# Two-step transfers, whole left slabs and a projection in 64x64 tiles, in a two-layer banded convolution kernel

## The chip, the cores and the metric

The kernel runs on one core of a Trainium2 chip. The metric is the device time of one execution in microseconds (us); lower is better. A core has five engines that run side by side, each through its own list of instructions in order: TensorE (PE, matrix products into PSUM), VectorE (DVE), ScalarE (ACT), GpSimd (POOL) and SyncE (SP, which here issues nearly all DMA transfers). They meet at semaphores only. SBUF is the on-chip memory with 128 partitions; x, the output and some intermediate arrays are in DRAM.

## The reference

x has the shape 1 x 512 x 512 x 64, float32. Two layers of the same form follow each other. Cut to what matters, one layer is (written as `_ln` for a normalization over the last axis, here without scale and bias since these are folded into weights):

```python
xn = _ln(x)                                             # over 64 channels
left  = (xn @ Wl + bl) * mask * sigmoid(xn @ Wlg + blg)  # 128 hidden channels
right = (xn @ Wr + br) * mask * sigmoid(xn @ Wrg + brg)
gate  = sigmoid(xn @ Wog + bog)
out[i, j] = sum over d = -4..4 of left[i + d, i] * right[i + d, j]
out = _ln(out) * gate
result = out @ Wo + bo
```

`left` is needed only in a band of nine entries around the diagonal. Around the layers the whole function also has a group normalization of the layer's input (statistics over the whole picture) and a residual, so that each layer reads its input twice: once as z, to be normalized, and once as XR, to which the result is added.

## The kernel before, in words

**Blocks and steps.** The 512 rows are cut into nine overlapping blocks of 64 rows (56 or 60 of them are kept, `blk.m`). The columns of a block are worked in two halves at once: partitions 0 to 63 hold the block's rows for a column of the left half, partitions 64 to 127 the same rows for a column of the right half. One step takes 8 columns of each half (`JU`), 16 steps make a chunk (`NU`), 18 chunks a layer, so a layer has 288 steps and 30 more in which its pipeline runs empty. In the function `layer` a step's item list (`FIRST` for the first layer, `SECOND` for the second) says in which order each engine gets its work; nothing is reordered inside an engine.

**One step.** z (128 partitions x 8 columns x 64 channels) is loaded two steps or more ahead (`load`), scaled and moved by the group normalization and centred (POOL), its row statistics are taken (DVE), it is transposed on PE (`transposed`, bank <- ident,z) and copied from PSUM to a tile `zT` on ACT (`kept`, line 477). `zT` has two buffers. It is used twice. First in the next step by PE for the projection to `right` (`crossed`, line 507; zT and pack are its operands): ACT makes the sigmoid of the gate half (`sg`) and DVE multiplies it into `RO`, the array of right. Second, `zT` is stored to DRAM (`later`), and read back as `zg` for the output gate of the step 30 further on. The band product (`mix`, RO and A as operands, output again to RO) has an operand A, a slab of 16 hidden channels of left that is fetched from DRAM (`take_left`, line 586); three slab buffers exist. A layer has as many band products as steps; within 16 steps they stand in the first ten, one or two a step. Then come the statistics of the band result (DVE), the normalization (`on`, ACT and two or fewer columns on POOL), its transposition, the gate (zg, pack -> `gate`, ACT), the product with it (`times_gate`, to `ZH`, DVE), the last product (`end`, PE), the sum with XR (`ended`, DVE), and the store. In the first layer PE also sums the results for the next group normalization (`sums`, acc <- XR).

**PE's tiles.** PE runs these products in different divisions of its array, which the profile prints as rows*columns: the gate, the projection and both transpositions in 64*128 (two products side by side), the last product and the sums in 128*64, the band products in 64*64 (four side by side). An f32 product shows as two matmul records, a transposition as one.

**What crosses in the projection.** `crossed` exchanges the two column halves for every second pair of 64 hidden channels, so that the band product finds its operands in the right partitions. It does so by reading `zT` from column 64 on for s = 1; for this `kept` writes the first 64 columns of each 192-column group a second time (the third third, `to[:, 2]`).

**Transfers.** All of them are issued by SP, in order, one after another: per step z (2 transfers, `load` line 405), later (1), zg (1), XR (2, `fetch` line 764), store of the result (2, `ended` line 788), and four for a slab A in every second step on average. In the first layer also some that prepare the left array (`left_of`). Eight completion semaphores are used in turn, so that a transfer is issued only when the one eight places before it has landed. One transfer moves 64 or 128 rows; `later` reads pieces of 512 B from zT, A and XR are moved in pieces of 512 B, z and zg in pieces of 2 KB.

Of the kernel before, what the change touches and what calls it, by code (L numbers as in the profile page):

```python
# [17 lines left out]
P = 128  # L18
# [86 lines left out]
def tile_two_banded_layers(  # L105
# [39 lines left out]
    ones_row = const.tile([1, P], F32, name="ones_row")  # L145
    nc.vector.memset(ones_row, 1.0)
# [93 lines left out]
    def solve_layer(i: int, f: dict, r: dict, tmp, half: bass.AP):  # L240
# [10 lines left out]
        for nm, lo, hi in (("right", 0, 2), ("left", 2, 4), ("gate", 4, 5)):  # L251
# [7 lines left out]
            en.vector.tensor_tensor(r[nm], aug[:, lo:hi], pm, ALU.subtract)  # L259
            en.vector.tensor_tensor(r[nm], r[nm], pb, ALU.add)  # L260
# [56 lines left out]
    both = const.tile([P, 2 * D], F32, name="both")  # L317
    total = const.tile([P, G], F32, name="total")

    fewer = const.tile([P, 2 * D], F32, name="fewer")  # L320
# [8 lines left out]
    def input_stats(meanwhile):  # L329
# [4 lines left out]
        with tc.tile_pool(name="gnx", bufs=3) as gx, tc.tile_pool(name="gns", bufs=1) as gs:  # L334
# [24 lines left out]
            tot = total  # L359
# [34 lines left out]
    zp = ctx.enter_context(tc.tile_pool(name="zp", bufs=11))  # L394
# [10 lines left out]
    def load(src: bass.AP, u: Unit):  # L405
        u.z = zp.tile([P, JU, D], F32, tag="z", name="z")
        if u.near is None:
            rows = slice(u.blk.s, u.blk.s + S)
            for e, j in enumerate((u.j, LH + u.j)):
                en.sync.dma_start(u.z[e * S : (e + 1) * S], src[rows, j : j + JU, :])  # L410
            return
        spans = [(0, u.near, u.near + JU)]
# [64 lines left out]
    def kept(u: Unit):  # L477
        u.t = ztp.tile([P, JU // 2, P + S], F32, tag="zT", name="zT")
        to = u.t.rearrange("c k (n p) -> c n k p", n=3)
# [106 lines left out]
    def take_left(n: int, h: int) -> bass.AP:  # L586


        A = lp.tile([P, HA // 2, S, 2], F32, tag="A", name="A")
        q = HA // 4  # L590
        for e in range(2):
            for s in range(2):
                en.sync.dma_start(
                    A[e * S : (e + 1) * S, s * q : (s + 1) * q].rearrange("p h i t -> p h (i t)"),
                    strided(
                        left_of, n * size + (s * H // 4 + h * q) * span + 2 * WIN,
                        (H // 2 * span, S), (span, q), (1, 2 * S),
                    ),
                )
        return A  # L600
# [37 lines left out]
    def solve(w: dict, ins: list, outs: list, sti, sto) -> dict:  # L638
# [3 lines left out]
        r = sm.tile([P, 3 * NB], F32, tag="rs", name="rs", bufs=3)[:, :n]  # L642
# [12 lines left out]
        def temporary(tag: str):  # L655
            return sm.tile([P, 3 * NB], F32, tag=tag, name=tag, bufs=1)[:, :n]
# [71 lines left out]
    def gated(o: Out):  # L728
        b = o.blk
        n = 2 * JQ * b.m  # L730
# [6 lines left out]
        o.g = g[:, : 2 * n].rearrange("h (x n p) -> h n x p", n=2, p=b.m)  # L737
# [14 lines left out]
    def times_gate(o: Out, w: dict):  # L752
        b = o.blk
        for n, pt in enumerate(o.pt):
            en.vector.scalar_tensor_tensor(
                ZH[(2 * o.n + n) % len(ZH)][:, :, : b.m], pt[:, :, b.lo : b.hi], w["ob"],
                o.g[:, n], ALU.add, ALU.mult,
            )

    def rows_of(v: bass.AP, o: Out, e: int):  # L760
        b, j = o.blk, e * LH + o.j
        return v[b.s + b.lo : b.s + b.hi, j : j + JU, :].rearrange("p (k t) c -> p k (t c)", t=2)

    def fetch(src: bass.AP, o: Out, w: dict, n: int):
        o.n, o.xr = n, XR[n % len(XR)]
        for e in range(2):
            en.sync.dma_start(o.xr[e * S : e * S + o.blk.m, :, 1 : 1 + 2 * D], rows_of(src, o, e))

    def biased(o: Out, w: dict):
        n = S + o.blk.m  # L770
        f = o.xr[:n, :, 1 : 1 + 2 * D]
        add = fewer if o.blk.m < S - WIN else both
        en.gpsimd.tensor_tensor(f, f, mid(add[:n], JU // 2), ALU.add)

    def end(o: Out, w: dict):
        po = one_bank().rearrange("i (j c) -> i j c", c=D)
        for k in range(JQ):
            for e in range(2):
                for n in range(2):
# [3 lines left out]
                        lhsT=ZH[(2 * o.n + n) % len(ZH)][:, e * JQ + k, :], rhs=w["Wo"],  # L783
# [4 lines left out]
    def ended(dst: bass.AP, o: Out):  # L788
        m, po = o.blk.m, o.po
        f = o.xr[: S + m, :, 1 : 1 + 2 * D]  # L790
# [3 lines left out]
        for e in range(2):  # L794
            en.sync.dma_start(rows_of(dst, o, e), o.xr[e * S : e * S + m, :, 1 : 1 + 2 * D])
# [13 lines left out]
    def layer(src: bass.AP, dst: bass.AP, w: dict, stats: bool, then=None):  # L809
# [64 lines left out]
        early = [u for t in sorted(loads) for u in loads[t] if u.near is None and u.at < 7]  # L874
        for u in early:
            load(src, u)
# [275 lines left out]
```

## Time and profile before

| | |
|---|---|
| time, median of 3 runs | 4618.48 us (4608.68 to 4629.22) |
| the profiled execution's own time | 4606.09 us |
| its span, first to last instruction | 4603.0 us |
| PE / its weight loads / DVE / ACT / POOL busy | 85% / 72% / 87% / 78% / 71% |
| DMA packets | 1,453,100, 988.15 MB, mean 215 GB/s |
| of them under 2 KB | 1,301,224 |
| SP's DMA queue | 1,447,360 packets, 974.41 MB, 78.0% of 16 engines' span |

The busy time of an engine is the time in which one of its instructions runs; a wait before an instruction is printed with what ended it (the releaser). The windows view cuts the span into stretches and gives the busy time and the number of instructions of each engine in each, the clock that PE was granted (1.00 is full), the share of the 16 DMA engines that was busy, and GB/s. The timeline lists instructions in order of time, merged where they are alike; SPq are SP's issues of transfers. Line 387 is that of a helper through which all instructions of the two layers are recorded, so work is told apart by the names of the tiles.

### The profile page before, as it was taken

The page shows a single profiled execution, that of the slowest core. Times are in us where ns is not written, and L with a number is a line of the kernel's source. Part 1 is how long each engine was busy: PE and PEld are TensorE (multiplying, and loading weights), DVE is VectorE, ACT ScalarE, POOL GpSimd, SP SyncE. Part 2 cuts the span into 40 slices and gives each one's busy share as a digit, 9 for nine tenths or more (in the row PEclk, how much of TensorE's full clock was granted, in tenths as well). Part 3 has the DMA queues.
Part 4 walks back from the last instruction along what each step waited for, and adds up shares of the span by engine and source line. Part 5 has one row for each costly group of instructions (what it writes and reads, how often), then busy time and mean ns, then how long its engine had stood idle before and what let it go on. Part 6 is the DMA issues. An engine that isn't in the chain of part 4 may idle for free. (4 is left out here: it accounts for less than half of the span.)

```text
span 4603.0 us, 192683 instructions
## 1 busy us (share of the span) xinstructions
PE 3891.6 (85%) x76306; PEld 3323.9 (72%) x76306; DVE 4004.6 (87%) x10943; ACT 3598.4 (78%) x8410; POOL 3284.6 (71%) x3427
## 2 busy tenths in 40 slices
PE   0146899999999999999985689998889898989998
PEld 0045788878787878887864578777777777777776
DVE  6976888888888888898877689999999999999998
ACT  0024898989898989898984478888888888888887
POOL 0047888888888888888723688777777777777741
PEclk9978999999999999999997899999999999999999
DMA  7837788888888798888863678888888888888876
GB/s 306 327 99 178 214 218 224 222 232 218 231 219 229 216 232 218 217 221 215 217 180 103 149 197 226 221 224 219 222 222 227 219 224 223 220 222 222 222 211 182
DMA packets 1453100, 988.15 MB, mean 215 GB/s; under 512 B 184002, under 2 KB 1301224, under 8 KB 1449192
## 3 DMA queue, kind: packets, MB, share of 16 engines
q1 hardware_dynamic: 1447360, 974.41, 78.0%
q8 instruction: 603, 9.88, 0.9%
q14 instruction: 297, 2.43, 0.2%
q10 hardware_dynamic: 4840, 1.43, 0.1%
HBM read 679.58 MB, written 317.11 MB: 217 GB/s over the span
## 5 line engine op out<-in xcount | busy, mean ns | idle before, releaser
L387 ACT ACTIVATE on<-RO,nm,rs 128x128 f32<-128x128 f32 x3744 | 1589.6, 493 | 86.7 <-DVE nm L387 48.0
L387 PEld LDWEIGHTS banks<-pack,zT 64*128 64x128 f32 x18576 | 1268.4, 198 | 410.6 <-ACT zT L387 260.9
L387 PE MATMUL banks<-pack,zT 64*128 64x128 f32 x18576 | 1324.6, 288 | 193.0 <-ACT zT L387 164.8
L387 DVE TENSOR_TENSOR RO<-banks,sg 128x512 f32<-128x512 f32 (+1 forms) x1188 | 794.2, 676 | 264.5 <-ACT sg L387 233.0
L387 ACT ACTIVATE sg<-banks 128x512 f32<-128x512 f32 (+1 forms) x1188 | 694.5, 592 | 246.7 <-PE banks L387 227.4
L387 POOL TENSOR_TENSOR z<-z,ga 128x512 f32<-128x512 f32 x536 | 682.4, 1281 | 195.9 <-DMA z<-mid_x 179.8
L387 DVE BATCH_NORM_STATS2 sto<-RO 128x6 f32<-128x256 f32 x2304 | 803.0, 411 | 0.8
L387 POOL TENSOR_SCALAR on<-RO,rs,nm 128x128 f32<-128x128 f32 x864 | 387.6, 456 | 566.3 <-ACT sg L387 298.0
L387 DVE SCALAR_TENSOR_TENSOR ZH<-bank,pack,gate 128x448 f32<-128x448 f32 (+1 forms) x1152 | 738.7, 683 | 44.0 <-ACT gate L387 25.3
L387 PE MATMUL bank<-zg,pack 64*128 64x448 f32 (+1 forms) x2304 | 730.7, 602 | 25.1 <-ACT RO L387 13.1
L387 PE MATMUL bank<-pack,ZH 128*64 128x64 f32 x18432 | 671.5, 226 | 16.7 <-DVE nm L387 15.7
L387 POOL TENSOR_TENSOR z<-z,gb 128x512 f32<-128x512 f32 x536 | 678.1, 1279 | 5.1
L387 POOL TENSOR_TENSOR z<-z,rs 128x512 f32<-128x512 f32 x586 | 619.2, 1057 | 70.2 <-DVE rs L387 42.4
L387 POOL TENSOR_TENSOR z<-z,sti 128x512 f32<-128x512 f32 x586 | 626.9, 1070 | 21.6 <-DVE sti L387 21.6
L387 ACT ACTIVATE zT<-banks 128x512 f32<-128x512 f32 (+1 forms) x1084 | 463.1, 478 | 224.1 <-DMA later<-zT 158.4
L387 PEld LDWEIGHTS bank<-pack,ZH 128*64 128x64 f32 x18432 | 591.5, 139 | 59.5 <-DVE nm L387 21.1
L387 ACT ACTIVATE gate<-bank 128x448 f32<-128x448 f32 (+1 forms) x1152 | 563.9, 542 | 9.4 <-PE bank L387 6.2
L387 DVE BATCH_NORM_STATS2 sti<-z 128x6 f32<-128x128 f32 x2344 | 503.4, 281 | 2.0 <-POOL z L387 1.9
L387 PE MATMUL bank<-ident,on 64*128 64x64 f32 x9216 | 455.3, 227 | 30.2 <-ACT gate L387 27.4
L387 PEld LDWEIGHTS bank<-ident,on 64*128 64x128 f32 x9216 | 426.7, 141 | 73.4 <-ACT gate L387 48.2
L387 DVE TENSOR_TENSOR XR<-bank,XR 120x512 f32<-120x512 f32 (+1 forms) x576 | 390.3, 678 | 6.9 <-POOL XR L387 3.0
L387 PE MATMUL banks<-ident,z 64*128 64x64 f32 x4336 | 252.3, 235 | 128.6 <-DVE RO L387 74.9
(151 smaller groups left out, 4044.4 us busy)
## 6 DMA issues: line engine op xcount, KB each, us to landing
later<-zT SPq DMA_DIRECT2D x576, 256.0 KB
A<-left_of SPq DMA_DIRECT2D x1152, 128.0 KB
zg<-later SPq DMA_DIRECT2D x576, 256.0 KB
z<-in_x_dram SPq DMA_DIRECT2D x576, 128.0 KB
z<-mid_x SPq DMA_DIRECT2D x576, 128.0 KB
gn_x<-in_x_dram SPq DMA_DIRECT2D x16, 4096.0 KB
XR<-in_x_dram SPq DMA_DIRECT2D x448, 112.0 KB
mid_x<-XR SPq DMA_DIRECT2D x448, 112.0 KB
```

Source lines behind the costliest of these rows:

```text
L387: return lambda *a, **k: tc.keep_in_program_order(f(*a, **k))
```

## The change

The program keeps its order of work on PE, DVE, ACT and POOL. What is different:

1. z is loaded for two steps at once: 16 columns, 4 KB pieces, half as many transfers. The pool holds six double tiles in place of eleven single ones. A pair is loaded at the earlier one of its two due times.
2. A slab of left is stored and read as one piece of 4,608 B per row, with the 8 unused columns at its edges, by two transfers in place of four. For this the hidden channels of left are put into another order when its weights are prepared (`by_slab`).
3. `kept` writes each transposed column once; `zT` has 128 columns per group in place of 192, and lies in one piece per partition, so that `later` moves 2 KB pieces.
4. `crossed` therefore works in 64x64 tiles: each product with 128 columns of zT becomes two with 64, and the crossing is done by the place of the output.
5. The gate's sigmoid goes straight to `ZH`, and `times_gate` multiplies in place; the tile `gate` is gone. `ZH` has two double buffers in place of four single ones.
6. XR and the result are moved for two steps at once, in three double buffers in place of four single ones: 4 KB pieces in the second layer, still 512 B pieces in the first, whose XR has a column of ones beside each 128 values. The store for two steps is issued at the end of the second.
7. Small tiles are shortened; `both` and `fewer` hold 64 columns and are read repeatedly by `biased`.

On SP, at the ninth and tenth step of a 16-step chunk of the first layer, before (each row is a kind of transfer with the shape of its destination and its count; `left_of<-left_of` prepares the left array of a later block):

```order
L387 DMA z<-in_x_dram 64x512 x2
L387 DMA XR_964<-in_x_dram 56x4x128 x2
L387 DMA A<-left_of 64x4x128 x4
L387 DMA left_of<-left_of 16x9216
L387 DMA later<-zT 512x1x128
L387 DMA mid_x<-XR_966 56x4x128 x2
L387 DMA zg<-later 128x512
L387 DMA XR_965<-in_x_dram 56x4x128 x2
L387 DMA A<-left_of 64x4x128 x4
L387 DMA later<-zT 512x1x128
L387 DMA mid_x<-XR_963 56x4x128 x2
L387 DMA zg<-later 128x512
```

The same two steps on SP with the change (`mid_x` is the first layer's result):

```order
L396 DMA z<-in_x_dram 64x1024 x2
L396 DMA A<-left_of 64x1152 x2
L396 DMA left_of<-left_of 16x9216
L396 DMA later<-zT 128x512
L396 DMA mid_x<-XR_955 56x8x128 x2
L396 DMA zg<-later 128x512
L396 DMA XR_957<-in_x_dram 56x8x128 x2
L396 DMA A<-left_of 64x1152 x2
L396 DMA later<-zT 128x512
L396 DMA zg<-later 128x512
```

The 23 transfers of the two steps have become 15: one XR fetch and one store of two transfers each serve both steps, and a slab takes two transfers.

On PE, in a step of the first layer with two band products, from the transposition of z on to that of `on`, before:

```order
L387 MATMUL banks<-ident,z 128x64 x8
L387 MATMUL banks<-RO,A 64x128 x16
L387 MATMUL acc<-XR_963 64x65 x8
L387 MATMUL banks<-RO,A 64x128 x16
L387 MATMUL bank<-zg,pack 128x448 x2
L387 MATMUL banks<-pack,zT 128x2x64 x16
L387 MATMUL bank<-ident,on 128x64 x16
```

The same place on PE with the change:

```order
L396 MATMUL banks<-ident,z 128x64 x8
L396 MATMUL banks<-RO,A 64x128 x16
L396 MATMUL acc<-XR_956 64x65 x8
L396 MATMUL banks<-RO,A 64x128 x16
L396 MATMUL bank<-zg,pack 128x448 x2
L396 MATMUL banks<-pack,zT 64x2x64 x32
L396 MATMUL bank<-ident,on 128x64 x16
```

Nothing has moved; the projection is 32 products with outputs of 64 partitions in place of 16 with 128, between two groups whose outputs have 128 partitions.

On ACT, one step (two sigmoids `sg`, the normalization `on`, the copies to `zT`, the gate), before:

```order
L387 ACTIVATE sg<-banks 128x512 x2
L387 ACTIVATE on<-RO,nm,rs 128x128 x4
L387 ACTIVATE zT<-banks 128x2x4x64
L387 ACTIVATE zT<-banks 128x4x64
L387 ACTIVATE on<-RO,nm,rs 128x128 x3
L387 ACTIVATE gate<-bank 128x448 x2
```

One step on ACT with the change:

```order
L396 ACTIVATE sg<-banks 128x512 x2
L396 ACTIVATE on<-RO,nm,rs 128x128 x4
L396 ACTIVATE zT<-banks 128x2x4x64
L396 ACTIVATE on<-RO,nm,rs 128x128 x3
L396 ACTIVATE ZH_967<-bank 128x4x2x56 x2
```

The second copy to zT is gone, and the gate is written to `ZH` in pieces of 56.

The core of the diff:

```diff
-    zp = ctx.enter_context(tc.tile_pool(name="zp", bufs=11))
+    zp = ctx.enter_context(tc.tile_pool(name="zp", bufs=6))
...
+    def load(src: bass.AP, *us: Unit):
+        two = zp.tile([P, 2 * JU, D], F32, tag="z", name="z")
+        for n, u in enumerate(us):
+            u.z = two[:, n * JU : (n + 1) * JU]
...
+        for e, j in enumerate((u.j, LH + u.j)):
+            en.sync.dma_start(two[e * S : (e + 1) * S], src[rows, j : j + 2 * JU, :])
...
     def kept(u: Unit):
-        u.t = ztp.tile([P, JU // 2, P + S], F32, tag="zT", name="zT")
+        u.t = ztp.tile([P, JU // 2, P], F32, tag="zT", name="zT")
...
         if u.near is None:
-            en.scalar.activation(
-                to[:, 2], u.pt[0][:, 0].rearrange("c (k p) -> c k p", p=S), AF.Identity, bias=1.0
-            )
-            en.sync.dma_start(later[u.at], u.t[:, :, :P])
+            en.sync.dma_start(later[u.at], u.t)
...
             for s in range(2):
-                for e in range(2):
-                    part = slice(e * D, (e + 1) * D)
-                    en.tensor.matmul(
-                        pr[:, e, k, :].rearrange("p (g s x) -> p g s x", g=2, s=2)[:, :, s],
-                        lhsT=u.t[part, q // 2 + k, s * S : s * S + P],
-                        rhs=w[part].rearrange("c (g s x) -> c g s x", g=2, s=2)[:, :, s],
-                        start=True, stop=True,
-                    )
+                for n in range(2):
+                    for e in range(2):
+                        part = slice(e * D, (e + 1) * D)
+                        to = slice((n ^ s) * S, (n ^ s) * S + S)
+                        en.tensor.matmul(
+                            pr[to, e, k, :].rearrange("p (g s x) -> p g s x", g=2, s=2)[:, :, s],
+                            lhsT=u.t[part, q // 2 + k, n * S : (n + 1) * S],
+                            rhs=w[part].rearrange("c (g s x) -> c g s x", g=2, s=2)[:, :, s],
+                            start=True, stop=True,
+                        )
...
-        A = lp.tile([P, HA // 2, S, 2], F32, tag="A", name="A")
-        q = HA // 4
+        wide = HA // 2 * span
+        A = lp.tile([P, wide], F32, tag="A", name="A")
         for e in range(2):
-            for s in range(2):
-                en.sync.dma_start(
...
+            en.sync.dma_start(
+                A[e * S : (e + 1) * S],
+                strided(left_of, n * size + h * wide, (H // 2 * span, S), (1, wide)),
+            )
...
-        g = gp.tile([H, 4 * JQ * (S - WIN)], F32, tag="gate", name="gate")
+        g = ZH[o.n % 2].rearrange("h n x p -> h x n p")[:, :, :, : b.m]
         for e, pg in enumerate(o.pg):
             en.scalar.activation(
-                g[:, e * n : (e + 1) * n].rearrange("h (k p) -> h k p", p=b.m), pg, AF.Sigmoid
+                g[:, e * JQ : (e + 1) * JQ], pg.rearrange("h (k n) p -> h k n p", n=2), AF.Sigmoid
             )
...
+            g = ZH[o.n % 2][:, n, :, : b.m]
             en.vector.scalar_tensor_tensor(
-                ZH[(2 * o.n + n) % len(ZH)][:, :, : b.m], pt[:, :, b.lo : b.hi], w["ob"],
-                o.g[:, n], ALU.add, ALU.mult,
+                g, pt[:, :, b.lo : b.hi], w["ob"], g, ALU.add, ALU.mult
             )
...
+    def both_of(o: Out, stats: bool, e: int) -> bass.AP:
+        part = slice(e * S, e * S + o.blk.m)
+        if stats:
+            return o.two[part, :, 1 : 1 + 2 * D]
+        return o.two[part].rearrange("p k c -> p (k c)")[:, : 2 * JU * D]
...
+    def fetch(src: bass.AP, o: Out, then: Out, n: int, stats: bool):
+        two = XR[n // 2 % len(XR)]
...
         for e in range(2):
-            en.sync.dma_start(o.xr[e * S : e * S + o.blk.m, :, 1 : 1 + 2 * D], rows_of(src, o, e))
+            en.sync.dma_start(both_of(o, stats, e), shaped(rows_of(src, o, e), stats))
...
-        for e in range(2):
-            en.sync.dma_start(rows_of(dst, o, e), o.xr[e * S : e * S + m, :, 1 : 1 + 2 * D])
+        if of is not None:
+            for e in range(2):
+                en.sync.dma_start(shaped(rows_of(dst, of, e), stats), both_of(of, stats, e))
...
-            if t + 1 in outs:
-                fetch(src, outs[t + 1], w, t + 1)
+            if t + 1 in outs and (t + 1) % 2 == 0:
+                fetch(src, outs[t + 1], outs[t + 2], t + 1, stats)
...
-                    ended(dst, p)
+                    ended(dst, p, outs[t - 2] if t % 2 == 0 else None, stats)
```

More of the change, by code (lines that the diff above doesn't have):

```diff
@@ L872, in layer @@
                 inners.setdefault(ahead[t] + 1, []).append((t, u))
-        early = [u for t in sorted(loads) for u in loads[t] if u.near is None and u.at < 7]
-        for u in early:
-            load(src, u)
+        first_of, pairs = {}, []
+        for t in sorted(loads):
+            for u in loads[t]:
+                near = u.near is not None
+                key = (near, (u.near if near else u.at * JU) // (2 * JU))
+                if key not in first_of:
+                    first_of[key] = []
+                    pairs.append((t, first_of[key]))
+                first_of[key].append(u)
+        loads = {}
+        for t, us in pairs:
+            loads.setdefault(t, []).append(sorted(us, key=lambda u: (u.near or 0, u.at)))
+        early = [us for t in sorted(loads) for us in loads[t] if us[0].near is None and us[0].at < 8]
+        for us in early:
+            load(src, *us)
         yield
@@ L884, in layer @@
                 recall(outs[t + 3])
-            for u in loads.get(t, []):
-                if u not in early:
-                    load(src, u)
-            if t + 1 in outs:
-                fetch(src, outs[t + 1], w, t + 1)
+            for us in loads.get(t, []):
+                if us not in early:
+                    load(src, *us)
+            if t + 1 in outs and (t + 1) % 2 == 0:
+                fetch(src, outs[t + 1], outs[t + 2], t + 1, stats)
             for c, h in slabs.get(t, []):
@@ L1093, in tile_two_banded_layers @@
     L9 = RO[:, :, 2 * JC - JW - NEAR * JQ :, :]
-    XR = [keep.tile([P, JU // 2, 2 * D + 2], F32, name=f"XR{i}") for i in range(4)]
+    XR = [keep.tile([P, JU, 2 * D + 2], F32, name=f"XR{i}") for i in range(3)]
     for t in XR:
@@ L1099, in tile_two_banded_layers @@
             nc.vector.memset(t[:, :, at : at + 1], 1.0)
-    ZH = [keep.tile([H, 2 * JQ, S], F32, name=f"ZH{i}") for i in range(4)]
+    ZH = [keep.tile([H, 2, 2 * JQ, S], F32, name=f"ZH{i}") for i in range(2)]
     for t in ZH:
```

83 lines of the change are left out of this document (46 added, 37 removed).

## The prediction, made before the changed kernel ran

> **What bounds the kernel now.** I read the windows first, cut at the borders of the two layers (columns: stretch, its length, busy time and number of instructions of PE, PEld, DVE, ACT and POOL, granted clock, DMA share, GB/s). The chain that ended last covers only the final 27 us of the span and says nothing of the steps.
>
> ```profile
> 0.00:262.00 262.00, 24.77 (x56) 12.76 (x56) 216.15 (x688) 2.09 (x4) 8.39 (x16) 1.00 0.73 291
> 262.00:476.00 214.00, 141.31 (x1977) 122.90 (x1978) 138.03 (x379) 98.72 (x228) 144.04 (x127) 0.79 0.59 143
> 476.00:2309.00 1833.00, 1734.65 (x35833) 1500.66 (x35831) 1604.59 (x4357) 1647.11 (x3872) 1548.44 (x1520) 0.99 0.84 222
> ...
> 2497.00:2697.00 200.00, 130.09 (x1971) 116.86 (x1968) 137.70 (x376) 93.34 (x217) 137.94 (x126) 0.82 0.58 140
> 2697.00:4460.00 1763.00, 1602.01 (x31722) 1380.45 (x31722) 1643.25 (x4451) 1517.30 (x3517) 1365.98 (x1519) 0.97 0.84 222
> ```
>
> The same windows with zT's instructions alone:
>
> ```profile
> 476.00:2309.00 1833.00, 556.06 (x8192) 543.88 (x8192) 217.87 (x512) 0.99 0.84 222
> 2697.00:4460.00 1763.00, 570.62 (x8192) 549.77 (x8192) 218.56 (x512) 0.97 0.84 222
> ```
>
> A projection has 32 matmul records, so each of the two steady stretches holds 8192/32 = 256 steps: 7.16 us a step in the first layer, 6.89 in the second. PE is busy 95% of the first, DVE 93% of the second (6.42 us a step).
>
> What a step needs on PE alone is read from PE's timeline (start, length, tile, count):
>
> ```profile
> 999.74 1.15 PE L387 MATMUL bank<-pack,ZH 128*64 128x64 f32 x32
> ...
> 1011.61 1.15 PE L387 MATMUL bank<-pack,ZH 128*64 128x64 f32 x32
> ...
> 1013.08 1.14 PE L387 MATMUL banks<-RO,A 64*64 64x128 f32 x32
> 1014.15 0.69 PE L387 MATMUL acc<-XR 120*64 120x65 f32 x16
> 1014.77 1.02 PE L387 MATMUL bank<-zg,pack 64*128 64x448 f32 x4
> 1015.62 1.95 PE L387 MATMUL banks<-pack,zT 64*128 64x128 f32 x32
> 1017.41 0.66 PE L387 MATMUL bank<-ident,on 64*128 64x64 f32 x16
> 1018.00 1.15 PE L387 MATMUL bank<-pack,ZH 128*64 128x64 f32 x32
> 1019.08 0.46 PE L387 MATMUL banks<-ident,z 64*128 64x64 f32 x8
> 1019.47 0.69 PE L387 MATMUL acc<-XR 120*64 120x65 f32 x16
> 1020.09 1.24 PE L387 MATMUL bank<-zg,pack 64*128 64x448 f32 x4
> ```
>
> From gate to gate, without a band product and without a wait, 1020.09 - 1014.77 = 5.32 us. A band product adds 1014.15 - 1013.08 = 1.07, and there is one a step on average: 6.39 us. So 0.77 us of each first-layer step is lost. The timeline of all engines shows how, around 1000 us; SPq are the issues of transfers:
>
> ```profile
> 994.12 3.74 SPq L387 DMA_DIRECT2D A<-left_of  x4
> 997.90 0.62 SPq L387 DMA_DIRECT2D left_of<-left_of  x1
> 998.62 0.55 SPq L387 DMA_DIRECT2D later<-zT  x1
> 999.26 1.12 SPq L387 DMA_DIRECT2D mid_x<-XR  x2
> 1000.50 1.60 SPq L387 DMA_DIRECT2D zg<-later  x1
> 1002.22 1.37 SPq L387 DMA_DIRECT2D z<-in_x_dram  x2
> 1003.64 1.02 SPq L387 DMA_DIRECT2D XR<-in_x_dram  x2
> 1004.76 0.58 SPq L387 DMA_DIRECT2D later<-zT  x1
> ...
> 1004.78 0.87 ACT L387 ACTIVATE zT<-banks 128x512 f32<-128x512 f32 x2 [3.13 <-DMA later<-zT]
> 1005.70 0.69 PE L387 MATMUL banks<-RO,A 64*64 64x128 f32 x16 [2.73 <-ACT zT L387]
> ```
>
> SP issues 13 transfers back to back between 994.12 and 1004.71, 10.02 us of issuing in 10.6; the store of zT comes late, ACT waits 3.13 us for the buffer and PE 2.73 us for ACT. From last product to last product that step took 1011.61 - 999.74 = 11.87 us; with its two band products it needs 5.32 + 2 x 1.07 = 7.46. The stall costs 4.4 us, more than the wait, since PE runs at a lower clock after it. How often this happens, and what else waits, is in the waits view (total, times, longest), first of the whole span, then of the first and the second steady stretch:
>
> ```profile
> ACT zT L387 <- DMA later<-zT: 200.7, 86, 11.2
> ...
> ACT zT L387 <- DMA later<-zT: 75.0, 32, 5.1
> DVE bank L387 <- ACT bank L387: 42.6, 13, 5.2
> PE banks L387 <- DVE RO L387: 16.7, 41, 0.8
> PE bank L387 <- DVE nm L387: 14.9, 31, 0.6
> PE banks L387 <- POOL on L387: 11.8, 14, 0.8
> ...
> POOL z L387 <- DMA z<-mid_x: 171.3, 56, 6.3
> ACT zT L387 <- DMA later<-zT: 75.4, 43, 3.5
> DVE bank L387 <- ACT bank L387: 37.8, 20, 3.8
> ```
>
> 75.0 us are 24 waits of 3.13 us; at 4.4 us each they cost 106 us, 0.41 us a step. PE's other waits for DVE and POOL are 43.4 us, 0.17 a step; 0.19 stay unexplained. So the first layer is bound by PE plus a stall that SP makes, the second by DVE plus late z and late zT.
>
> **The change part by part.**
>
> *Transfers.* On average a step issues 10 transfers (z 2, later 1, zg 1, A 2, XR 2, result 2) and afterwards 6. The quoted stretch of 13 would be 8 (A 2, left 1, later 1, result 1, zg 1, z 1, XR 1). At the 0.77 us that one took there (10.02/13) that is 6.2 us in place of 10.0, under a step's 7.16. If a transfer of twice the size takes twice as long to issue, nothing is gained; but an issue of later, with 512 pieces, takes 0.55, and a z with 64 takes about 0.7, so neither pieces nor bytes set it, and I take the first. Their pieces grow too. At the start, where the statistics read large pieces, 291 GB/s took a share of 0.73, or 399 GB/s of a full share; the steady stretches reach 222/0.84 = 264. A first-layer step moves 222 GB/s x 7.16 us = 1.59 MB, so the engines' 6.0 us a step fall to no less than 4.0. I expect both waits for DMA to go nearly wholly: 0.41 us a step in the first layer. The Trainium skill ("DMA: Bandwidth & Descriptors", Specifications) has 512 B as the least size for line rate; by that the larger pieces would give nothing, and only the fewer issues would be left. The two windows above do not agree with it.
>
> *Copy to zT.* One ACT instruction of 0.37 us goes from each step:
>
> ```profile
> L387 ACT ACTIVATE zT<-banks 128x256 f32<-128x256 f32 x542 | 200.8, 370 | 0.0
> L387 POOL TENSOR_TENSOR z<-z,ga 128x512 f32<-128x512 f32 x536 | 682.4, 1281 | 195.9 <-DMA z<-mid_x 179.8 <-DMA z<-in_x_dram 12.4 <-PE bank L387 3.5
> L387 POOL TENSOR_TENSOR XR<-XR,fewer 120x512 f32<-120x512 f32 x224 | 266.2, 1188 | 110.7 <-DMA XR<-in_x_dram 66.1 <-DVE rsqrt_t L387 17.2 <-DVE bank L387 10.6
> ```
>
> ACT falls from 1647.11/256 = 6.43 to 6.06 us a first-layer step. It is not the bound, so I count nothing for it by itself; it helps ACT to be ahead of PE.
>
> *Projection.* 32 records become 64. Beside each other in 64*64 tiles the band products show the rate. Doubling a count gives the part that doesn't grow: the last product's 32 records take 1019.08 - 1018.00 = 1.08 us, the sums' 16 of nearly the same form 1020.09 - 1019.47 = 0.62; 16 cost 0.46, and 0.16 is what it costs to go into another division of the array and out. A band's 32 then take 1.07 - 0.16 = 0.91, 28.4 ns each, and 64 take 1.82 us against 1.79 now (1017.41 - 1015.62): +0.03. But gate, projection and `on` now stand in one division, 64*128, and the projection leaves it: two more switches, 2 x 0.16 = **0.32 us a step** on PE. Bounds: 0 if the loads of weights hide them, 0.32 as for every other group in these rows. I take 0.32, so PE needs 6.39 + 0.35 = 6.74 us in the first layer. In the second, without the sums' 0.62, it needs 5.32 - 0.62 + 1.07 + 0.35 = 6.12, less than DVE's 6.42.
>
> *The rest.* ACT writes the gate in shorter pieces, twice a step: no gain is to be had from that, and with 6.92 - 6.06 = 0.86 us of ACT idle each could take 0.43 longer before it counts. DVE's in-place product reads and writes as many elements as before: 0. `biased` on POOL now repeats 64 values, as z<-z,ga does, which takes 1281 ns and not 1188: between 0 and 0.09 us a step, beside 285 us of idle POOL in the first layer. A pair of z is loaded earlier than its second half needs, and by the planner's due times 32 of 144 loads come in the step whose transpositions free their buffer (67 of 288 before): no change taken; its price is in the third rival.
>
> *Sum.* First layer: if all that was lost goes, 6.74; if only the 0.41 goes, 7.16 - 0.41 + 0.35 = 7.10. I take the middle, 6.92, since DVE's 42.6 us waiting for ACT belong to the same stalls, and PE's waits for DVE follow when DVE catches up: 0.24 x 256 = -61 us. Second layer: DVE's 6.42 at best, 6.89 if other waits take over; I take 6.62, nearer to DVE's own work because 37.8 us of its idle time again hang on late zT and z is late by 171.3 us on POOL: -0.27 x 256 = -69 us. In the two fillings (262 to 476, 2497 to 2697) and the ends lie 200.7 - 75.0 - 75.4 = 50 us of waits for later; I take 15 of these 0 to 50. Together -145 us from 4606.09, the profiled execution's own time (span 4603.0): **4461 us**. The median of the runs, 4618.48, lies 0.3% above that execution, inside the runs' spread, so I leave it at that.
>
> **Rivals.**
>
> *Relief without gain.* The transfers come early, but DVE, ACT and POOL take the wait's place: 7.10 us in the first layer (-15 us), 6.85 in the second (-10), fillings as before: about 4580 us. For it: in the second layer DVE is at 93%, and PE's switches are new. Against it: the stalled step is 4.4 us long, and DVE stands idle in it.
>
> *Tile order in the projection (slower).* The band products go round the four tiles; the new projection does not: for s = 0 it takes two tiles twice removed, then for s = 1 the last pair again at once. If PE can't look past a tile that is still busy, tiles stand empty. Three of four in use would make 64 x 28.4 x 4/3 = 2.42 us, +0.60; over 512 steps +307 us, of which the second layer's slack of 6.42 - 6.12 = 0.30 takes 77: 4461 + 230 = **4690 us**. It decides from 145/512 = 0.28 us a step on, with that slack from about 0.4. Nothing in the trace repeats a tile so early, so this is open. The Trainium skill ("TensorE: Matmul & The Clock Gate", Part 3, The mechanism) says that matmuls start and end strictly in program order. By that, the two passes of each f32 product would keep two tiles at work at most: 64 records at 1.79/32 = 56 ns, 3.58 us, far over 4690 in sum. The band row speaks against it: 32 records in 0.91 us are four at a time.
>
> *Pairs that hold SP up.* If a load that waits for its pair's buffer makes later late, two such steps in 16, at 4.4 us each over 32 groups of 16 steps, give +282 us: 4740 us. Half as many issues behind it speak against.
>
> **How the numbers follow.** The forecast, 4400 to 4560: 0.58. A larger gain, towards 4461 - 47 - 51 - 35 = 4330 with every low end: 0.10. Relief without gain, 4560 to 4630: 0.20. Tile order: 0.08. Pairs: 0.04. The range 4370 to 4610 leaves out the lower half of the larger gain, the tip of the relief case and both slow rivals, about 0.2. A measurement of this kernel can tell about 0.5% from no change, so 4595 is the border: faster 0.58 + 0.10 + half of 0.20 = 0.78, within 0.5% 0.10, slower 0.12.
>
> **What would show it.** Right: ACT's wait for later nearly gone, SP with gaps, the projection at about 1.8 us at full clock, gate to gate without a band 5.6 us, first-layer steps near 6.9, second near 6.6 with DVE at 97%. Wrong: a projection over 2.1 us (tile order), the zT wait still there (transfers), or no wait for DMA and steps of 7.1 and 6.9 (relief without gain).

## The result, and the profile after

The changed kernel takes 4787.57 us (median, 4772.11 to 4802.43) against 4618.63 us before: the ratio is 1.0365, with an interval of 1.0324 to 1.0407. It is slower by 3.65%, where 3.4% faster was forecast, and outside the range.

The windows of the changed kernel, cut into the same stages (columns as before: stretch, length, PE, PEld, DVE, ACT, POOL busy, granted clock, DMA share, GB/s):

```profile
262.00:480.00 218.00, 126.52 (x2783) 104.79 (x2785) 131.21 (x359) 79.36 (x172) 137.56 (x120) 0.81 0.56 137
480.00:2443.00 1963.00, 1820.28 (x44250) 1442.36 (x44246) 1622.72 (x4380) 1619.85 (x3642) 1551.40 (x1527) 0.98 0.84 213
...
2640.00:2850.00 210.00, 126.91 (x2792) 107.75 (x2796) 129.17 (x357) 79.08 (x173) 131.68 (x119) 0.77 0.53 130
2850.00:4660.00 1810.00, 1661.37 (x40004) 1312.83 (x39994) 1653.57 (x4455) 1458.07 (x3270) 1363.82 (x1522) 0.98 0.83 222
```

From the starts of the gates, 1963 us are 258 steps and 1810 us are 256: **7.61 us** a first-layer step (before 7.16) and **7.07** a second-layer step (before 6.89), so 116 and 46 us of the 198 us between the two profiled spans are in the steady stretches, the rest in the two fillings, which take 16 and 23 us longer up to the layer's first gate. PE is busy 93% of the first stretch, 95 before; in the second it has overtaken DVE (92% and 91%).

What it waits for is in the waits view of the changed kernel (total, times, longest):

```profile
PE banks L396 <- issue: 107.8, 90, 3.8
...
PE bank L396 <- issue: 92.5, 72, 3.3
...
ACT zT L396 <- DMA later<-zT: 89.2, 16, 14.6
...
PE acc L396 <- issue: 10.8, 9, 2.5
```

The same view of the kernel before has these rows of PE:

```profile
PE banks L387 <- issue: 0.5, 1, 0.5
...
PE bank L387 <- issue: 0.2, 1, 0.2
```

The wait that the change was to remove is gone from the steady stretches: ACT's wait for the store of zT, 75 us in each of them before, is in neither now, and what is left of it (89.2 us, 16 times) lies in the fillings. POOL's wait for a late z, 171.3 us in the second layer, is 1.5 us. A new one has come: 107.8 + 92.5 + 10.8 = **211 us**, 171 waits, in which PE waits on "issue", that is, for nothing that the profile shows. (A further row, two waits of 8.7 us at L255, lies in the preparation before the first step and is not counted, here or below.) The timeline of the changed kernel around one of them (start, length, engine, tile, count; SPq issues transfers):

```profile
1069.33 1.02 PE L396 MATMUL bank<-zg,pack 64*128 64x448 f32 x4
...
1070.28 1.98 PE L396 MATMUL banks<-pack,zT 64*64 64x128 f32 x62
...
1074.28 0.79 SPq L396 DMA_DIRECT2D zg<-later  x1
1075.12 1.22 SPq L396 DMA_DIRECT2D z<-in_x_dram  x2
1076.01 0.19 PEld L396 LDWEIGHTS banks<-pack,zT 64*64 64x64 f32 x2 [4.00 <-issue]
1076.02 0.43 PE L396 MATMUL banks<-pack,zT 64*64 64x128 f32 x2 [3.76 <-issue]
...
1076.48 0.60 ACT L396 ACTIVATE sg<-banks 128x512 f32<-128x512 f32 x1 [4.35 <-PE banks L396]
...
1077.18 0.69 DVE L396 TENSOR_TENSOR RO<-banks,sg 128x512 f32<-128x512 f32 x1 [4.33 <-ACT sg L396]
```

Products are counted from here on as the profile prints them, as matmul records, of which an f32 product has two; each record has its own load of weights (LDWEIGHTS). PE stops after 62 of the 64 records of one step's projections, whose operands were all there with the first, and does the last two 3.8 us later. No semaphore is involved, and ACT and DVE then wait for PE. The table of DMA queues tells what PE lacks. Of the changed kernel (packets, MB, share of 16 engines):

```profile
q1 hardware_dynamic: 667072, 993.14, 77.5%
q8 instruction: 746, 12.22, 1.1%
```

and before:

```profile
q8 instruction: 603, 9.88, 0.9%
```

A packet of q8 has 12.22 MB / 746 = 16 KB. PE's loads and matmul records are 2 x 76306 before and 2 x 94738 now (the page's first part), and both are close to 256 for each packet of q8; with the 1599 semaphore waits and the like in PE's list it is 191,075/746 = 256.1 now. So q8 brings **PE's instructions**, 256 at a time. Counted in the order of that list, all 171 stops fall on the same two neighbouring places of the 256 in such a block. In the stopped step above, the last packet of q8 landed at 1074.64, and PE went on at 1076.01.

### The profile page after: what moved, and what is told of

It reads as the page before. It is cut to its first block, busy times and chain, and to the rows that moved or that the text cites. A ratio compares the mean times of both kernels' runs of the same rounds, so it can differ in the third digit from the quotient of the medians.

```text
span 4800.6 us, 224234 instructions
## 1 busy us (share of the span) xinstructions
PE 4018.9 (84%) x94738; PEld 3170.3 (66%) x94738; DVE 4024.1 (84%) x10942; ACT 3478.9 (72%) x7834; POOL 3276.4 (68%) x3425
## 3 DMA queue, kind: packets, MB, share of 16 engines
q8 instruction: 746, 12.22, 1.1%
## 5 line engine op out<-in xcount | busy, mean ns | idle before, releaser
L396 PEld LDWEIGHTS banks<-pack,zT 64*64 64x64 f32 x37008 | 1084.2, 138 | 604.6 <-issue 248.4
L396 PE MATMUL banks<-pack,zT 64*64 64x128 f32 x37008 | 1258.5, 281 | 206.8 <-ACT zT L396 93.5
L396 DVE SCALAR_TENSOR_TENSOR ZH<-bank,pack,ZH 128x448 f32<-128x448 f32 (+1 forms) x1152 | 739.5, 683 | 85.8 <-PE bank L396 57.1
L396 PE MATMUL bank<-pack,ZH 128*64 128x64 f32 x18432 | 689.1, 228 | 51.3 <-issue 41.0
L396 PE MATMUL bank<-zg,pack 64*128 64x448 f32 (+1 forms) x2304 | 698.8, 605 | 13.4 <-DVE ZH L396 5.0
L396 ACT ACTIVATE ZH<-bank 128x448 f32<-128x448 f32 (+1 forms) x1152 | 564.5, 540 | 20.4 <-PE bank L396 18.6
L396 PE MATMUL bank<-ident,on 64*128 64x64 f32 x9216 | 434.0, 231 | 59.6 <-issue 31.5
L396 PEld LDWEIGHTS bank<-ident,on 64*128 64x128 f32 x9216 | 346.6, 140 | 190.6 <-issue 98.1
L396 ACT ACTIVATE zT<-banks 128x512 f32<-128x512 f32 x542 | 315.1, 581 | 106.4 <-PE banks L396 99.2
L396 PE MATMUL banks<-RO,A 64*64 64x128 f32 x9216 | 345.4, 282 | 35.4 <-issue 24.6
```

The source lines that it names most:

```text
L396: return lambda *a, **k: tc.keep_in_program_order(f(*a, **k))
```

## The experiments

The theory, called **supply**: PE has two blocks of 256 instructions at most; the next is asked for when it enters its last one (98% of the fetches begin only then), and has to land before PE is through with that. Two things became worse at once: 64 more instructions a step (32 records and their loads), so that PE is through sooner, and a fetch that takes longer, since it stands behind the data that SP has issued. Rivals: the order of tiles in the new projection, the length of the pieces, the number of instructions alone. Each ratio below is to the kernel before on the same chip.

**Undo the projection alone.** In the changed kernel the projection takes the one copy of zT in 64*128 tiles. Both halves take it uncrossed, so the second half of each projection is not the reference's.

```diff
-                for n in range(2):
-                    for e in range(2):
+                for e in range(2):
...
-                            lhsT=u.t[part, q // 2 + k, n * S : (n + 1) * S],
+                        lhsT=u.t[part, q // 2 + k, 0 : P],
```

> The changed kernel with the projection in 64*128 tiles again (32 records, not 64), from the one kept copy: the second half of each product isn't crossed over, so the output isn't the reference's. Theory supply (PE runs out of instructions: 128 more load and product records a step less 64, and long data pieces ahead of the fetch): PE's waits on issue fall from about 200 us to under 50, first-layer steps to 6.9 and second to 6.6, in all 4400 to 4500. Rival long pieces alone (the fetch is late because of the pieces, however many instructions): waits on issue stay over 150 us, about 4620 to 4700. Rival other parts of the change (gates in place, pairs): about 4750.

Measured: 4543.47 us, ratio 0.9825 [0.981, 0.9839]. The waits of this kernel:

```profile
PE banks L396 <- issue: 26.6, 25, 3.3
PE bank L396 <- issue: 23.4, 25, 1.9
...
PE acc L396 <- issue: 3.4, 5, 1.4
```

A quarter of 211 us, 53 us, is left, just over the 50 that supply had as its bound, and the time is 43 us over its range; the direction is that of supply. Long transfers alone do not starve PE as the change does.

**Do the projection alone.** The kernel before with the changed `kept` and `crossed`, its transfers untouched.

> The kernel before with the one-copy zT and the 64x64 projection alone; its transfers stay in short pieces. Theory supply: more instructions, but fetches land as fast as before, so PE's waits on issue stay under 60 us; two more switches a step cost 0.28 us in the first layer and less in the second: 4640 to 4740. Rival instructions alone (the count starves PE whatever the pieces): waits on issue near 200 us again, 4800 to 4900. Rival tile order: the projection itself is over 2.1 us and the waits stand inside it.

Measured: 4608.78 us, ratio 0.9968 [0.9953, 0.9984], slightly faster than before and below every theory's range. Its waits:

```profile
ACT zT L387 <- DMA later<-zT: 173.3, 76, 11.5
POOL z L387 <- DMA z<-mid_x: 167.2, 57, 5.9
...
PE acc L387 <- issue: 2.0, 1, 2.0
...
PE bank L387 <- issue: 0.7, 1, 0.7
PE banks L387 <- issue: 0.6, 2, 0.3
```

The same instructions as the changed kernel, and 3.3 us of waits on issue. So neither their number nor the order of tiles does it alone. That the two switches cost nothing here, where late transfers still set many steps, fits; it was not tested by itself. Alone, the projection brings -0.3% and the rest -1.75%; together they give +3.65%. The loss is in what the two parts do to each other.

**Shorter pieces, first the slabs.** The changed kernel, whose slabs come in two transfers as before, cut to the window on the way:

```diff
-                A[e * S : (e + 1) * S],
-                strided(left_of, n * size + h * wide, (H // 2 * span, S), (1, wide)),
+                A[e * S : (e + 1) * S].rearrange("p h i t -> p h (i t)"),
+                strided(
+                    left_of, n * size + h * HA // 2 * span + 2 * WIN,
+                    (H // 2 * span, S), (span, HA // 2), (1, 2 * S),
+                ),
```

> The changed kernel with the left slabs fetched in pieces of 512 B in place of 4608 B (same two transfers a slab, from the same stored order, the window cut while loading). Theory supply with long pieces: the fetch of instructions lands sooner, PE's waits on issue fall from about 200 us to under 80, 4600 to 4690. Rival instructions alone or tile order: 4760 to 4800, waits on issue unchanged.

Measured: 4778.16 us, ratio 1.0341 [1.0318, 1.0364], waits on issue 198 us: my expectation missed, and the time is the one of its rival, the number of instructions or the tile order, which the kernel just above rules out. I had taken slabs for the cause because the late fetches fall on them; it isn't the length of their pieces. The last rival, the length of all pieces, was tried later, with slabs, pairs of z and the store of zT in the pieces of before (slabs cut as above, the others padded), in the same six issues:

```diff
-        two = zp.tile([P, 2 * JU, D], F32, tag="z", name="z")
+        two = zp.tile([P, 2, JU * D + 2], F32, tag="z", name="z")[:, :, : JU * D]
...
-        u.t = ztp.tile([P, JU // 2, P], F32, tag="zT", name="zT")
+        u.t = ztp.tile([P, JU // 2, P + 2], F32, tag="zT", name="zT")[:, :, :P]
```

> The changed kernel with the same six issues a step and the same pairs, but pieces as short as before: slabs in 512 B, z in 2 KB, the store of zT in 512 B. Theory backlog: pieces don't matter, the mean backlog stays near 570 KB, PE's waits on issue stay at 180 to 220 us, 4750 to 4800. Rival long pieces: the fetches land as soon as before, waits on issue under 60 us, 4600 to 4680.

Measured: 4742.14 us, ratio 1.0286 [1.0255, 1.0317]. Its waits:

```profile
PE banks L396 <- issue: 96.5, 98, 3.0
...
PE bank L396 <- issue: 70.5, 73, 3.1
```

176 us with `acc`: the rival is out, though time and waits lie a little below supply's ranges too. Shorter pieces, with 11% fewer bytes for the slabs, take about a fifth of the loss with them.

**Half of the products back.** The uncrossed half in 64*128, the crossed one in 64*64: 48 records a step.

```diff
-        for k in range(JQ // 2):
-            for s in range(2):
-                for n in range(2):
+        for s in range(2):
+            for k in range(JQ // 2):
+                for n in range(1 + s):
...
+                        to = slice((n ^ s) * S, (n ^ s) * S + S) if s else slice(0, P)
+                        of = slice(n * S, (n + 1) * S) if s else slice(0, P)
```

> The changed kernel with the uncrossed half of the projection in 64*128 tiles and the crossed half in 64*64: 48 records in place of 64, still two switches more than before. Theory supply: 32 load and product records a step fewer, waits on issue fall to about half (60 to 120 us), 4640 to 4720. Rival switches or tile order (cost set by leaving the division, not by the count): 4740 to 4790.

Measured: 4779.54 us, ratio 1.0345 [1.0311, 1.0378], the rival's time; but its waits on issue are 60 us, as supply had them:

```profile
PE banks L396 <- issue: 30.8, 33, 2.5
...
PE bank L396 <- issue: 21.9, 23, 2.2
...
PE acc L396 <- issue: 6.9, 10, 1.2
```

The edit had a cost that I overlooked: each of the two projections of a step now changes the division twice. From gate to gate without a band the best steps take 5.97 us, against 5.60 in the changed kernel and 5.32 before, some 0.3 us for every two switches. Two effects of like size cancelled, and the time alone would have misled.

**Same bytes, more issues.** The changed kernel, each wide transfer of z, A, XR and the results issued in two halves at the same place, for instance:

```diff
-            en.sync.dma_start(two[e * S : (e + 1) * S], src[rows, j : j + 2 * JU, :])
+            for i in range(0, 2 * JU, JU):
+                en.sync.dma_start(
+                    two[e * S : (e + 1) * S, i : i + JU], src[rows, j + i : j + i + JU, :]
+                )
```

> The changed kernel with each wide transfer of z, A, XR and the results issued in two halves at the same place: same bytes, same buffers, same stored order, pieces of 2 KB to 2.3 KB, 10 to 11 issues a step. Theory backlog (the fetch of PE's instructions waits behind the data that SP has issued and that hasn't moved yet; with fewer issues SP runs ahead and the mean backlog rose from 335 to 592 KB): SP is paced again, mean backlog under 450 KB, PE's waits on issue fall from 211 us to under 60, waits for late transfers come back, 4590 to 4680. Rival paired bursts (what counts is how many bytes one step asks for): backlog and waits on issue stay, 4750 to 4800.

Measured: 4637.86 us, ratio 1.0028 [1.001, 1.0045]. Its waits:

```profile
ACT zT L396 <- DMA later<-zT: 204.2, 71, 15.3
...
PE banks L396 <- issue: 4.8, 5, 3.5
...
PE bank L396 <- issue: 1.0, 2, 0.7
PE acc L396 <- issue: 0.8, 2, 0.6
```

Nearly all of the loss is gone, by doing what the change had removed. With more issues SP paces the DMA engines; with six a step it runs ahead and stands waiting for the next zT, 895 us in the changed kernel against 168 here and 99 before (SP's own waits for ACT's zT). One might say that PE, held up here by the store of zT, only uses its instructions more slowly; but the median block of 256 takes it 5.2 us here, less than the 5.6 of the changed kernel with its stops, and the fetch lands in 2.3 us in place of 3.1 (table below). Moving work in time, without an issue more, does part of it: the changed kernel with the slabs' loads behind the step's store of zT,

```diff
-            for c, h in slabs.get(t, []):
-                A[c, h] = take_left(c // per, h)
...
                 elif name == "keep":
...
+                    for c, h in slabs.get(t, []):
+                        A[c, h] = take_left(c // per, h)
```

> The changed kernel with the two loads of a slab A issued after the step's store of zT, not at the start of the step with zg, z and XR. Theory backlog: the burst at the start of a step shrinks by 576 KB, so fetches land sooner; waits on issue fall from 211 us to 80 to 150, 4640 to 4740. Rival paired bursts or count alone: unchanged, 4760 to 4800. A slab that comes late would show as a wait of PE for A.

Measured: 4697.11 us, ratio 1.0141 [1.0112, 1.017], waits on issue 137 us, and no wait for a late A among its rows.

**What the changed transfers are worth with the old projection.** Two kernels that compute everything: the changed one with the three-part zT and the projection of before, and z in single steps, for space; and the same with the slabs cut as above.

```diff
-    zp = ctx.enter_context(tc.tile_pool(name="zp", bufs=6))
+    zp = ctx.enter_context(tc.tile_pool(name="zp", bufs=11))
...
-        u.t = ztp.tile([P, JU // 2, P], F32, tag="zT", name="zT")
+        u.t = ztp.tile([P, JU // 2, P + S], F32, tag="zT", name="zT")
```

> The changed kernel with the three-part zT and the 64*128 projection of before, and z loaded one step at a time as before, for space; it computes everything. Theory backlog: PE takes 256 instructions in 6.4 us as before and z no longer comes in 512 KB bursts, so the mean backlog is near 500 KB and waits on issue stay under 50 us: 4480 to 4550. Rival: the third copy on ACT brings the wait of zT for its store back (over 60 us in the steady stretches): 4580 to 4620.

> The same as the kernel just before it, with the left slabs cut to their window while they load (256 KB in place of 288 KB a transfer, pieces of 512 B). Theory backlog: 11% fewer bytes for A, pieces without effect, so 0 to 20 us less than that kernel. Rival: 512 B pieces cost the DMA engines more, 20 to 60 us more.

Measured: 4484.7 us, ratio 0.9694 [0.9676, 0.9712], and **4473.21 us, ratio 0.9668 [0.9649, 0.9687]**: 3.3% faster than before. The windows of the second:

```profile
465.00:2240.00 1775.00, 1716.04 (x35914) 1494.76 (x35915) 1607.58 (x4375) 1659.49 (x3891) 1551.49 (x1526) 1.00 0.95 230
2627.00:4331.00 1704.00, 1594.38 (x31890) 1386.99 (x31888) 1646.15 (x4473) 1521.51 (x3542) 1368.25 (x1528) 0.98 0.90 231
```

By its gates that is 6.89 us a first-layer step at full clock with PE busy 97%, and 6.62 with DVE at 97%. Two more edits of this kernel, each alone: the slabs behind the store of zT, and XR and results in single steps:

> The fastest kernel so far (old projection, single z, cut slabs; 4473 us) with the slabs' loads issued after the store of zT. Theory backlog: its waits on issue are small already, so at most 10 us are to be had: 4455 to 4480. Rival: A comes late (PE waits for A) or z does: 4490 to 4520.

> The fastest kernel so far (4473 us) with x and the results moved one step at a time again: 9 issues a step, not 7. Theory backlog with SP as the pacer: the mean backlog falls from 526 to about 400 KB, but SP is busy for over 6 us of a step and the wait of zT for its store grows by 20 to 60 us: 4480 to 4540. Rival: smoother transfers win, 4450 to 4470.

Measured: 4466.6 us, ratio 0.9689 [0.9668, 0.971], and 4464.98 us, ratio 0.9684 [0.9661, 0.9707]. Both are the same as 0.9668 within the intervals. The expected loss of the second did not come (its time is in the rival's range): the waits of zT for its store are 56 us, 50 without the edit.

**The new projection where transfers are no bound.** The kernel of 0.9668 with `kept` and `crossed` of the changed kernel; of the edit, the line of zT:

```diff
-        u.t = ztp.tile([P, JU // 2, P + S], F32, tag="zT", name="zT")
+        u.t = ztp.tile([P, JU // 2, P], F32, tag="zT", name="zT")
```

> The fastest kernel so far (4473 us) with the new projection (one copy, 64x64 tiles) in place of the old one. It cost nothing beside the old transfers (4609 beside 4625 us). Theory supply: here it costs 0.28 us a first-layer step for two switches (72 us), about 0.1 in the second (26 us), and 60 to 150 us of waits on issue, since 64 more instructions a step meet a backlog of 526 KB: 4600 to 4720. Rival switches alone: 4550 to 4580, waits on issue under 30 us.

Measured: 4593.53 us, ratio 0.9966 [0.9948, 0.9984], a little below supply's range, with 81 us of waits on issue and 7.26 and 6.71 us a step. The projection costs 3% of the time here, after nothing beside the old transfers. This kernel also differs from the one with short slab pieces in a single thing, the loads of z in single steps and not in pairs. That alone takes the ratio from 1.0341 to 0.9966, the waits on issue from 198 to 81 us and the start of the first gate from 477.8 to 460.6 us: the same bytes in smaller issues again.

**One table.** From the traces: the data backlog (bytes that SP has issued less those of finished packets, mean over the steady part), the median from PE's entering its last block to the landing of the next, the waits of PE on issue in us, and the ratio.

| kernel | records of the projection | backlog KB | fetch us | waits on issue | ratio |
|---|---|---|---|---|---|
| projection alone | 64 | 351 | 2.2 | 3.3 | 0.9968 |
| split issues | 64 | 382 | 2.3 | 6.6 | 1.0028 |
| new projection, single z | 64 | 491 | 2.9 | 81 | 0.9966 |
| slabs after store | 64 | 558 | 3.2 | 137 | 1.0141 |
| short pieces | 64 | 560 | 3.2 | 176 | 1.0286 |
| short slab pieces | 64 | 565 | 3.1 | 198 | 1.0341 |
| **the change** | 64 | 592 | 3.1 | 211 | 1.0365 |
| half of the products | 48 | 598 | 2.9 | 60 | 1.0345 |
| **before** | 32 | 335 | 1.9 | 0.7 | 1 |
| single x and results | 32 | 415 | 2.3 | 4.9 | 0.9684 |
| cut, after store | 32 | 482 | 2.5 | 4.6 | 0.9689 |
| cut slabs | 32 | 526 | 2.6 | 9.6 | 0.9668 |
| old projection, single z | 32 | 562 | 2.7 | 16 | 0.9694 |
| wide projection | 32 | 685 | 3.3 | 53 | 0.9825 |

With 64 records the waits grow with the backlog from 3 to 211 us; with 32, at 562 KB, they are 16 where 64 have 137 to 198, and even 685 KB bring no more than 53. The loss of the change takes both, more instructions and more backlog. Inside the changed kernel the fetch lands 2.1 us after PE enters its last block when under 250 KB are outstanding, and 4.9 us when 1000 to 1250 KB are; with short pieces it is 2.2 and 4.9. PE needs 5.6 us for 256 instructions (6.4 before), 4.4 in the quickest 5%, and takes up work some 1.4 us after a late block has landed.

## Why the prediction was wrong

- **The bound before: right in kind, too dear in the first layer.** Late zT and late z did cost time, and both waits are gone. Late zT was priced at 0.41 us of a first-layer step; in the kernel with cut slabs, which has the old projection and under 10 us of both waits in its steady stretches, a step is 7.16 - 6.89 = 0.27 us shorter.
- **Transfers: half right.** Six issues free SP, and the waits go, as forecast. The step counted an SP that runs ahead as gain only. That SP's slowness had kept the backlog at 335 KB, and that something else stands in the DMA engines behind the data, was not in it. This, with the instructions of the next step, is **the step that failed**: the transfers and the projection were summed as if they didn't touch each other, but the backlog went from 335 to 592 KB, the fetch of a block from 1.9 to 3.1 us, and PE's waits on issue from 0.7 to 211 us. A second error in it cost nothing: longer pieces did not shorten the DMA engines' work. 213/0.84 and 222/0.83 are 254 and 267 GB/s for a full share, 264 before; the 399 that the large pieces at the start suggested did not come. The rule that I weighed and set aside, 512 B as enough for line rate (the Trainium skill, "DMA: Bandwidth & Descriptors", Specifications), agrees with this trace. It agrees roughly: over the whole span the DMA queue of the kernel with short pieces moved 243 GB/s for a full share (974.27 MB at 84.5% of 4737.7 us), that of the changed kernel 267.
- **Projection: its time right, its instructions not counted.** It was to cost +0.03 for its rate and 0.32 for two switches. The timeline of the changed kernel has a step without band or wait:

```profile
1836.59 1.06 PE L396 MATMUL bank<-zg,pack 64*128 64x448 f32 x4
1837.59 1.98 PE L396 MATMUL banks<-pack,zT 64*64 64x128 f32 x64
1839.49 0.71 PE L396 MATMUL bank<-ident,on 64*128 64x64 f32 x16
...
1842.23 1.06 PE L396 MATMUL bank<-zg,pack 64*128 64x448 f32 x4
```

  1842.23 - 1836.59 = 5.64 us, against 5.32: +0.32. But 32 more records are 64 more instructions with their loads, and these were costed as PE's time alone. Of the 0.69 us between the forecast of 6.92 and 7.61, the waits view of that stretch has (70.7 + 36.2 + 10.8)/258 = 0.46 on issue. A little more is clock: after the stop shown above the granted clock is 0.5 for 3.4 us, from 1077.13 on, and in that stretch such times add up to 71 us, against 48 before; the difference is worth 12 us of full clock, 0.05 a step. The rest, 0.18, was not measured by itself.
- **Pairs: not free.** I took no change for loading z in pairs and -15 us for the fillings; they grew by 16 and 23. In the first filling ACT's wait for the store of zT went up, before and after:

```profile
ACT zT L387 <- DMA later<-zT: 24.8, 5, 9.7
```

```profile
ACT zT L396 <- DMA later<-zT: 43.2, 7, 14.4
```

  Pairs also raise the backlog: single steps alone brought the waits on issue from 198 to 81 us (above), and the prediction took nothing for this. With z in single steps the first gate came at 465.4 us or earlier in every kernel, with pairs at 476 us or later.
- **The sum.** 6.92 and 6.62 us a step, 4461 us, is what the transfers reach with the old projection (6.89, 6.62, 4473 us), where PE has 0.32 us less to do: the middle that I took was too low as well for a kernel with the switches. With them and little backlog the first layer has 7.19 and 7.25 (projection alone, split issues), which are bound by transfers, or 7.26 with 81 us of waits.
- **The rivals.** None named the mechanism. The projection's tile order costs nothing: its 64 records take 1.98 us, 1.95 for 32 before, not the 2.42 of that rival nor the 3.58 that was worked out for strict order. Pairs do hold zT's store up, but in the fillings alone.

The Trainium skill has this fetch ("Runtime: NRT & Kernel Launch", Instruction fetch mechanics): blocks of 16 KiB, 256 instructions, the next one loaded while the current one runs, at a cost "mostly hidden". The 16 KB packets agree; hidden it is before (0.7 us of waits) and not after (211 us).

## What to carry to other kernels

Count what a change adds in instructions, not only in engine time: where PE uses up 256 of them in 4 to 6 us, as here, their fetch is a transfer with a deadline like any other. Fewer and larger transfers took away the pacing by the issuing queue here, and the data then stood in front of that fetch; look at the backlog, not only at waits for data. Two parts that each gain can lose together, so try each alone before the sum is believed.

## What the runs showed that was not expected

- A stop of PE on "issue" in mid-group, with no semaphore, is a late block of instructions (all 171 stops here): 16 KB for 256 instructions, two blocks at most, so an f32 product, with two loads and two passes, uses four places.
- The fetch waits behind data that is issued and not yet moved: 2.1 us at under 250 KB, 4.9 us at 1000 to 1250 KB, whatever the length of the pieces.
- A change of PE's division costs 0.14 to 0.18 us at both places where one was added: about +0.3 us for two (5.60 to 5.64, less 5.32), +0.65 for four (5.97 - 5.32).
- Taking out ACT's second copy to zT saved less than the 0.37 us that it takes by itself: the two copies overlapped, and ACT was busy with them for 463.1/542 = 0.85 us a step before and for 315.1/542 = 0.58 now. The forecast of 6.06 us of ACT in a first-layer step was so too low (1619.85/258 = 6.28); ACT was not the bound, so it cost nothing. The copy of 128x512 itself takes 581 ns, 585 before.
